# A block's rows split into halves behind the search, and one of two row sets scaled on GpSimd from the other's transposed tiles

## The chip, the cores and the metric

The kernel runs on one core of a Trainium2 chip. The metric is the device time of one execution in microseconds (us). Engines: PE is TensorE (matmuls and transposes), ACT is ScalarE, DVE is VectorE, POOL is GpSimd, and SP is the engine whose queue issues most DMAs.

## The reference, cut to what matters

Layer 0 is a graph attention layer over 2708 nodes with 512 features; layer 1, which the change concerns, is a diffusion in two steps. With h the normalised output of layer 0:

```python
S = S + eye(n)
Rf = S / S.sum(axis=1, keepdims=True)        # rows by row sums
Rb = S / S.sum(axis=0)[:, None]              # the same rows by column sums
Xf = Xb = Xa = h
for s in range(2):
    A = adj_from_feats(Xa, W1, W2, W3)       # nucleus-filtered softmax rows
    Xf = Rf @ Xf
    Xb = Rb @ Xb
    Xa = A @ Xa
    Z = Z + (Xf @ U1[s] + Xb @ U2[s] + Xa @ U3[s])
```

`adj_from_feats` forms the logits of each row (a product with 2708 keys), finds for each row the threshold above which 90% of the softmax mass lies, and keeps only what is above it. In step 0, Xf and Xb start from the same h, so both are the one product S @ h, scaled row by row: by 1/row sum for Xf, by 1/column sum for Xb. Row t of Xb is therefore row t of Xf times (row sum / column sum).

## The kernel before, in words

The 2708 rows are 22 tiles of 128 (the last has 20), taken in 11 pairs (`pairs`); two pairs make a quad (`quads`, six, the last of two tiles). After layer 0 the loop `for s in range(STEPS)` (L914) runs the two diffusion steps. Within a step, the loop over g (L1183, from -1 to 10) is a software pipeline over the pairs. In iteration g there run:

- `lg[g+2].products()` (L513): the logits of pair g+2, on PE, copied from PSUM to the tiles p by ACT (L523);
- `search(lg[g+1])` (L598): on DVE alone, the threshold of pair g+1, in rounds of passes over p (L629), then `finish` (L798), which writes the masked rows `keep` (L730) and ends in a branch on a value read from a tile (L888 to L890). `keep` is the input of the next iteration's transposes;
- `attended(pairs[g])` (L1005): A @ Xa for pair g, in 12 steps n (two tiles, six groups of up to four key tiles). In each step PE transposes four blocks of `keep` (L1016), ACT copies them to `at` (L1020), and PE multiplies the group before (L1035);
- `mixed(pairs[g])` (L1060): the three products with U1, U2 and U3, n = 0, 1, 2, with four k each. `turned_rows` transposes the rows (L147 on PE, L149 on ACT) that the next n needs, so x0, x1 (Xf, Xb, loaded at L1001) and xa are each transposed once;
- `part(half, g+2)` (L943): the product S @ h of a quad, in step 0 spread over two iterations, 11 key tiles c in each. One `product(c)` is 8 matmuls (L967) and two loads. When the second half is done, that is in odd g, `scaled` runs eight times for the quad: ACT reads a PSUM bank q and scales it by rinv or cinv into xe (L977), POOL stores xe to xfb_d (L978), and in step 0 `split_rows` (L175) follows: DVE writes a high part and the rest into split_hl (L181, L182), and POOL stores it to fhl_d or bhl_d, from which step 1 reads.
- `exp` (L526) of pair g+2: after DVE's row maxima (L548), on ACT a first pass and the exponential of each tile (L553, L560), POOL's starting points (L565 to L575), then twelve "looks" (L553), ACT passes over p of 128x2708, and POOL's `masses` (L578 to L580), on which the next search waits (L646).

The order on PE, ACT, DVE and SP is written by hand (`manual_schedule`, L1164): each engine takes its instructions in the order in which the Python code makes them. The order on POOL is found by the scheduler. Two lists are spread over `attended` and `mixed`: `others` holds the steps of `part` (11 products, in odd g of step 0 the eight `scaled` after them, and the loads of `diffused`), `fills` the ACT work of `exp`. `paced(list, n)` runs the next n entries. In `attended`, step 0 runs `1 + i` entries of `others` in each step (i is 0 for the first tile of the pair, 1 for the second) and from step `first` on one or two of `fills`; `mixed` runs one of `others` for each k, and one of `fills` for k below 3 of n = 0 and 1. What is left of both runs after `mixed`. `late` (L1220), which holds `attended` and `mixed`, comes in the code before `finish(0)` (L904, L905): what it puts on DVE stands ahead of the end of the search.

Buffers that matter: xe has 4 buffers in step 0 and 2 in step 1, split_hl 2, the PSUM tiles t (transposes and logits) 2, the PSUM tiles a (attended and mixed) 2, q one for each of the quad's four tiles, u_k 3 in step 0.

Of the kernel before, what the change touches and what calls it, by code (L numbers as in the profile page):

```python
# [24 lines left out]
P = 128  # L25
# [28 lines left out]
def kernel(  # L54
# [58 lines left out]
    xfb_d = dram.tile([2, N, D], F32, name="xfb_d")  # L113
    xa_d = dram.tile([N, D], F32, name="xa_d")
    en_d = dram.tile([H, N], F32, name="en_d")
    rank_d = dram.tile([NT * P], BF16, name="rank_d")

    ident = const.tile([P, P], F32, name="ident")
# [6 lines left out]
    rinv = const.tile([P, NT], F32, name="rinv")  # L125
    cinv = const.tile([P, NT], F32, name="cinv")
    ratio = const.tile([P, NT], F32, name="ratio")

    def row_bcast(ap, n):
        return bass.AP(tensor=ap.tensor, offset=ap.offset, ap=[[0, P], [1, n]])  # L130
# [323 lines left out]
    for r, c0, c1 in [(P, 0, NFULL), (rows[-1], NFULL, NT)]:  # L454
        if c0 == c1:
            continue
        s = (slice(0, r), slice(c0, c1))
        for v, inv in ((rsum, rinv), (csum, cinv)):
            nc.vector.tensor_scalar(v[s], v[s], 1.0, 1e-12, op0=OP.add, op1=OP.max)
            nc.vector.reciprocal(inv[s], v[s])  # L460
        nc.vector.tensor_mul(ratio[s], cinv[s], rsum[s])

# [451 lines left out]
    for s in range(STEPS):  # L914
        last = s == STEPS - 1
        with ExitStack() as st:
# [26 lines left out]
            def part(half, b):  # L943

                if b // 2 >= len(quads):
                    return []
                quad = quads[b // 2]  # L950
                first = b % 2 == 0
                w = len(quad) * P
                hl_d = (fhl_d if first else bhl_d) if last else vhl_d
                cs = range(NT) if last else range(0, NT // 2) if first else range(NT // 2, NT)
                steps = []

                def product(c):
                    if c == 0:
                        half[:] = [ps_s.tile([P, D], F32, name=f"q{i}") for i in range(len(quad))]
                    hl = sp.tile([P, 2, D], F32R, name="hl", bufs=3)  # L960
                    nc.sync.dma_start(out=hl.bitcast(F32), in_=hl_d[c * P:(c + 1) * P])
                    s_r = sp.tile([P, 2 * G * P], F32R, name="s_r")
                    nc.sync.dma_start(out=s_r[:, :w].bitcast(F32),
                                      in_=s_d[c * P:(c + 1) * P, quad[0] * P:quad[0] * P + w])
                    for j in range(len(quad)):
                        for h in range(2):
                            nc.tensor.matmul(half[j], lhsT=s_r[:, j * P:(j + 1) * P], rhs=hl[:, h],  # L967
                                             start=(c == 0 and h == 0), stop=(c == NT - 1 and h == 1))

                def scaled(t, ps, i, inv, to):  # L970
                    pr = rows[t]

                    if last and b < 2 and t % 2:
# [3 lines left out]
                    nc.scalar.activation(x[:pr], ps[:pr], AF.Copy, scale=inv[:pr, t:t + 1])  # L977
                    nc.gpsimd.dma_start(out=xfb_d[i, cols[t], :], in_=x[:pr])  # L978
                    if not last:
                        split_rows(parts, nc.vector, x[:pr], t, to)  # L980

                steps += [lambda c=c: product(c) for c in cs]
                if last or not first:
                    for j, t in enumerate(quad):
                        if first or not last:
                            steps.append(lambda j=j, t=t: scaled(t, half[j], 0, rinv, fhl_d))
                        if not first:
                            steps.append(lambda j=j, t=t: scaled(t, half[j], 1, cinv, bhl_d))
                return steps

            def paced(steps, n):
                for step in steps[:n]:
# [1 line left out]
                del steps[:n]  # L994

            def diffused(grp):
                out_ = []
                for i in range(2):
                    for t in grp:
                        x = work.tile([P, D], F32, name=f"x{i}")  # L1000
                        nc.sync.dma_start(out=x[:rows[t]], in_=xfb_d[i, cols[t], :])  # L1001
                        out_.append(x)
                return out_[:len(grp)], out_[len(grp):]

            def attended(grp, keep, rden, fills, others, then, first=3):  # L1005

# [20 lines left out]
                for n, (i, t, cs) in enumerate(steps):  # L1027
                    pr = rows[t]
                    nxt = turned(*steps[n + 1]) if n + 1 < len(steps) else then()
                    if n >= first:  # L1030
                        paced(fills, 1 + i if last else 1 if n > 8 else 2)
                    if cs[0] == 0:
                        pa = ps_a.tile([P, D], F32, name="a")
                    for j, c in enumerate(cs):
                        nc.tensor.matmul(pa[:pr], lhsT=at[:rows[c], j, :pr], rhs=va[:rows[c], c, :],  # L1035
                                         start=(c == 0), stop=(c == NT - 1))
                    if not last:
                        paced(others, 1 + i)
                    elif i or len(grp) == 1:
                        paced(others, (total + 10) // 13)  # L1040
                    if cs[-1] == NT - 1:
                        xa.append(work.tile([P, D], F32, name="xa"))
                        nc.scalar.activation(xa[i][:pr], pa[:pr], AF.Copy, scale=rden[:pr, i:i + 1])  # L1043
# [16 lines left out]
            def mixed(grp, v_t, xf, xb, xa, others, fills, final=False):  # L1060

# [6 lines left out]
                    for i, t in enumerate(grp):  # L1068
                        project(small, ps_t.tile([P, 512], F32, name="t"), v_t[i], t, s + 1)
                for n, u in enumerate((u3, u1, u2) if final else (u1, u2, u3)):  # L1070
                    nxt = turned_rows(grp, ((xf, xb) if final else (xb, xa))[n]) if n < 2 else None
                    for k in range(KD):
                        u_k = up.tile([P, D], F32, name="u_k", bufs=4 if last else 3)
                        nc.sync.dma_start(out=u_k, in_=u[s, k * P:(k + 1) * P, :])  # L1074
# [89 lines left out]
            with tc.manual_schedule(engines={PE, ACT, DVE, SP}):  # L1164
# [12 lines left out]
                for step in part(half, 0):  # L1177
                    step()
                values()
                done = []  # L1180
                ready = None
                looks, left = [], []
                for g in range(-1, NP):  # L1183

                    fills = []

                    held = len(left)
                    paced(left, held if last else held // 2)
                    others = left + part(half, g + 2)
                    left = []  # L1190
                    if g == 0 and last:
                        paced(others, 4)
                    if g + 2 < NP:
                        lg[g + 2].products()
                    if g + 3 < NP:
# [4 lines left out]

                    rows_in = []
                    if g >= 0:
                        others.insert(0 if g else len(others) // 3, lambda g=g: rows_in.extend(diffused(pairs[g])))
                        final = g == NP - 1 and not last
                        att = attended(pairs[g], *ready, fills, others,
                                       lambda: None if final else turned_rows(pairs[g], rows_in[0]),
                                       3 if g else len(tgroups) + 1)
                    if g == 0:

                        paced(others, held - held // 2 if not last else 0)  # L1210
                        while looks:
                            next(att)
                            paced(looks, 2)

                    def early(g=g):
                        if g + 2 < NP:
# [3 lines left out]
                    def late(g=g):  # L1220
                        if g >= 0:
                            if g:
                                paced(others, 1)
                            xa, v_t = rest_of(att)
                            done.extend(mixed(pairs[g], v_t, *rows_in, xa, others, fills, final))
# [52 lines left out]
```

## Time and profile before

| | |
|---|---|
| time, median of 3 runs | 3710.2 us (3706.47 to 3715.27) |
| profiled execution, its own time | 3708.3 us |
| its span, first to last instruction | 3706.5 us |
| layer 0 | 0 to about 1080 us |
| step 0 of the diffusion | about 1080 to 2300 us |
| step 1 | about 2300 to 3706 us |
| busy PE / DVE / ACT / POOL | 3367.4 / 2612.9 / 1541.5 / 799.6 us |
| mean granted TensorE clock | 0.966 of full speed |

In the tables of groups a row gives the line, the engine, out<-in, the count, the busy time, the mean of one instruction, and the idle time of the engine before it with what ended it. In a timeline the first number is the start, the second the length, and the square bracket the idle time of that engine just before, with the instruction that released it. "DVEq L890" is DVE's branch at the end of a search.

### The profile page before, as it was taken

To read this page: it belongs to the slowest core of one execution; us is meant where nothing else is said; L and a number is where in the kernel's file an instruction comes from. 1 tells how busy PE (TensorE), PEld (TensorE's weight loads), DVE (VectorE), ACT (ScalarE), POOL (GpSimd) and SP (SyncE) were. 2 spreads that over 40 slices of the span, in tenths; PEclk is the share of its full clock that TensorE was granted. 3 is DMA by queue.
4 is the path that set the end of the run, shared out by engine and by line. 5 is a ranking of instruction groups with operands and counts; after the bars stand their busy time and mean duration, and the time that the engine had idled before them with its cause. 6 is when DMAs were issued, how large, how long until landed. Compare 5 with 4: busy or idle time off the path is not lost. (4 is left out here: it accounts for less than half of the span.)

```text
span 3706.5 us, 35338 instructions
## 1 busy us (share of the span) xinstructions
PE 3367.4 (91%) x11143; PEld 1754.4 (47%) x11143; DVE 2612.9 (70%) x4820; ACT 1541.5 (42%) x2334; POOL 799.6 (22%) x1119
## 2 busy tenths in 40 slices
PE   7998999998966988989899899688999999999898
PEld 4433333333444545545455453445655565556452
DVE  4588888889957637365463651969988779777991
ACT  2343212111114674655666612345654556445511
POOL 4114140514331112121202121302112111121101
PEclk9999999999978999999999999999999999999999
DMA  3477424233228445454535353966556665566552
GB/s 113 152 252 243 137 80 150 80 105 103 74 87 278 164 157 187 145 183 149 205 131 196 128 191 100 302 203 225 175 187 208 233 216 204 183 213 234 201 201 66
DMA packets 276459, 634.08 MB, mean 171 GB/s; under 512 B 37210, under 2 KB 70442, under 8 KB 273244
## 3 DMA queue, kind: packets, MB, share of 16 engines
q1 hardware_dynamic: 249183, 540.99, 44.2%
q0 software_dynamic: 27024, 90.30, 6.3%
q8 instruction: 89, 1.46, 0.2%
q14 instruction: 163, 1.33, 0.1%
HBM read 509.07 MB, written 122.10 MB: 170 GB/s over the span
## 5 line engine op out<-in xcount | busy, mean ns | idle before, releaser
L1035 PE MATMUL a<-va,at 128*128 128x512 f32 (+2 forms) x1936 | 890.1, 599 | 14.0 <-ACT at L1020 13.5
L967 PE MATMUL q<-hl,s_r 128*128 128x512 f32 x2904 | 820.9, 429 | 62.5 <-DMA s_r<-s_d 62.2
L429 PE MATMUL po<-e,fw 128*65 128x512 f32 (+4 forms) x2112 | 838.7, 552 | 34.3 <-DVE e L427 21.8
L427 DVE SCALAR_TENSOR_TENSOR e<-r_b,kk,a_c 128x512 f32<-128x512 f32 (+4 forms) x1056 | 751.8, 741 | 73.5 <-PE po L429 23.7
L967 PEld LDWEIGHTS q<-hl,s_r 128*128 128x128 f32 x2904 | 544.4, 190 | 307.5 <-issue 133.2
L553 ACT ACTIVATE junk_a<-p,nth 128x2708 uint8<-128x2708 f32 (+1 forms) x240 | 613.1, 2554 | 70.6 <-POOL nth L572 66.8
L429 PEld LDWEIGHTS po<-e,fw 128*65 128x65 f32 (+1 forms) x2112 | 286.2, 140 | 546.7 <-issue 269.2
L1035 PEld LDWEIGHTS a<-va,at 128*128 128x128 f32 (+2 forms) x1936 | 337.1, 187 | 379.4 <-issue 342.7
L1076 PE MATMUL a<-u_k,v_t 128*128 128x512 f32 (+1 forms) x1056 | 489.9, 601 | 22.3 <-ACT xa L1043 15.4
L629 DVE SCALAR_TENSOR_TENSOR junk<-p,th 128x2708 bf16<-128x2708 f32 (+1 forms) x132 | 401.2, 3039 | 4.0
L1020 ACT COPY at<-t 128x512 f32<-128x512 f32 (+3 forms) x308 | 140.4, 477 | 494.5 <-PE t L1016 494.1
L1076 PEld LDWEIGHTS a<-u_k,v_t 128*128 128x128 f32 (+1 forms) x1056 | 188.9, 187 | 242.1 <-issue 182.9
L521 PE MATMUL t<-keys,q_t 128*128 128x452 f32 x528 | 167.1, 443 | 118.4 <-ACT p L523 98.1
L181 DVE TENSOR_SCALAR split_hl<-xe 128x512 int32<-128x512 int32 (+1 forms) x44 | 19.1, 434 | 257.1 <-ACT xe L977 210.7
L808 DVE MAX8 vn<-keep 128x8 f32<-128x2708 f32 (+1 forms) x66 | 196.8, 2981 | 2.3
L523 ACT COPY p<-t 128x452 f32<-128x452 f32 (+2 forms) x264 | 132.0, 538 | 126.5 <-PE t L521 82.3
L521 PEld LDWEIGHTS t<-keys,q_t 128*128 128x128 f32 x528 | 91.7, 211 | 189.2 <-ACT p L523 150.7
L411 ACT ACTIVATE s_c<-a_c 128x512 fp32r<-128x512 f32 (+3 forms) x132 | 76.1, 577 | 247.5 <-DMA a_c<-in_adj_t_dram 120.7
L1016 PE MATMUL t<-ident,keep 128*128 128x128 f32 (+1 forms) x968 | 147.2, 274 | 27.1 <-DVE keep L757 19.2
L1016 PEld LDWEIGHTS t<-ident,keep 128*128 128x128 f32 (+1 forms) x968 | 115.0, 139 | 107.5 <-issue 79.5
L548 DVE TENSOR_REDUCE nmx<-p 128x1 f32<-128x2708 f32 (+1 forms) x44 | 129.0, 2966 | 41.7 <-ACT p L523 41.7
L565 POOL TENSOR_TENSOR x<-sums,powers 128x4 f32<-128x4 f32 x22 | 44.7, 2033 | 508.7 <-ACT p L560 508.7
(296 smaller groups left out, 3151.9 us busy)
## 6 DMA issues: line engine op xcount, KB each, us to landing
s_r<-s_d SPq DMA_DIRECT2D x330, 256.0 KB
hl<-vhl_d SPq DMA_DIRECT2D x132, 512.0 KB
u_k<-in_L_gnn_U_dram SPq DMA_DIRECT2D x264, 256.0 KB
hl<-fhl_d SPq DMA_DIRECT2D x132, 512.0 KB
hl<-bhl_d SPq DMA_DIRECT2D x132, 512.0 KB
arow<-in_adj_dram SPq DMA_DIRECT2D x21, 1354.0 KB
s_d<-s_c SPq DMA_DIRECT2D x88, 256.0 KB
a_c<-in_adj_t_dram SPq DMA_DIRECT2D x84, 256.0 KB
```

The lines of the kernel that those rows point to most:

```text
L427: nc.vector.scalar_tensor_tensor(e[:pr, :cw], r_b[:pr, i, :cw], kk[:pr, t, hd:hd + 1], a_c[t][:pr, :cw], op0=OP.max, op1=OP.mult)
L429: nc.tensor.matmul(po[i][:, :cw], lhsT=fw[:pr, t, hd, :], rhs=e[:pr, :cw], start=(t == 0), stop=(t == NT - 1))
L521: nc.tensor.matmul(pl[:, :c1 - c0], lhsT=q[:, i], rhs=self.keys[:, c0:c1], start=(i == 0), stop=(i == 1))
L523: nc.scalar.copy(p[:pr, c0:c1], pl[:pr, :c1 - c0])
L553: nc.scalar.activation(junk[:pr], self.p[i][:pr], func, **kw)
L629: v.scalar_tensor_tensor(junk_b[:pr], ps_[i][:pr], th, ps_[i][:pr], op0=OP.is_ge, op1=OP.mult, accum_out=dst)
L808: v.max(vs, keep[0][:pr])
L967: nc.tensor.matmul(half[j], lhsT=s_r[:, j * P:(j + 1) * P], rhs=hl[:, h], start=(c == 0 and h == 0), stop=(c == NT - 1 and h == 1))
L1016: nc.tensor.transpose(pt[:rows[c], j, :pr], keep[i][:pr, cols[c]], ident[:pr, :pr])
L1020: nc.scalar.copy(at[:r, j0:j1, :pr], pt[:r, j0:j1, :pr])
L1035: nc.tensor.matmul(pa[:pr], lhsT=at[:rows[c], j, :pr], rhs=va[:rows[c], c, :], start=(c == 0), stop=(c == NT - 1))
L1076: nc.tensor.matmul(pz[i][:rows[t]], lhsT=v_t[i][:, k, :rows[t]], rhs=u_k, start=(n == 0 and k == 0), stop=(n == 2 and k == KD - 1))
```

## The change

In step 0:

- Only Xf is stored to xfb_d and loaded again by `diffused`. The column-scaled rows xe of the second kind are still made, since they are split for step 1.
- Xb's transposed tiles are formed by a new helper, `times`: GpSimd multiplies Xf's transposed tiles by a row of ratios (row sum / column sum) that is broadcast to all partitions. The ratios are transposed once behind layer 0 (PE, ACT), stored to rat_d by SP, and loaded for each pair.
- `part` returns the products and the `scaled` entries apart, and `scaled` returns its split as a function that is called later. The first half of a quad's `scaled` entries run on ACT at the end of `mixed` in odd g (`half_scaled`), ahead of the copies yo; their splits run at the top of the next iteration, behind the search. The second half and its splits run there too, behind the next pair's logits and ahead of its search.
- The pacing in `attended` is one entry of `others` in two steps of three in place of `1 + i`; in even g from 2 on, `fills` begin at step 5 in place of 3, and the loads of `diffused` stand third in `others`. The rest of `others` runs in `mixed`.

In step 1 only one order changes: what is left of `others` after the last k now runs ahead of the copies yo (L1089) in place of behind them.

```diff
+    with tc.tile_pool(name="rat", bufs=1) as pool, tc.tile_pool(name="rat_ps", bufs=1, space=PSUM) as ps:
+        pt = ps.tile([NT, P], F32, name="ratio_t")
+        nc.tensor.transpose(pt, ratio, ident)
+        ratio_t = pool.tile([NT, P], F32, name="ratio_t")
+        nc.scalar.copy(ratio_t, pt)
+        nc.sync.dma_start(out=rat_d.rearrange("(t p) -> t p", p=P), in_=ratio_t)
...
-                    nc.gpsimd.dma_start(out=xfb_d[i, cols[t], :], in_=x[:pr])
-                    if not last:
-                        split_rows(parts, nc.vector, x[:pr], t, to)
+                    if last or i == 0:
+                        nc.gpsimd.dma_start(out=xfb_d[i, cols[t], :], in_=x[:pr])
+                    return lambda: None if last else split_rows(parts, nc.vector, x[:pr], t, to)
...
+                if not last:
+                    ratios = small.tile([P, G * P], F32, name="ratios")
+                    nc.sync.dma_start(out=ratios[:, :len(grp) * P],
+                                      in_=row_bcast(rat_d[grp[0] * P:(grp[-1] + 1) * P], len(grp) * P))
-                for i in range(2):
+                for i in range(2 if last else 1):
...
-                        paced(others, 1 + i)
+                        paced(others, 1 if n % 3 else 0)
...
+            def times(grp, v_t, ratios):
+                out_ = []
+                for i, t in enumerate(grp):
+                    pr = rows[t]
+                    x = up.tile([P, KD, P], F32, name="v_t")
+                    nc.gpsimd.tensor_tensor(x[:, :, :pr], v_t[i][:, :, :pr],
+                                            ratios[:, i * P:i * P + pr].unsqueeze(1).to_broadcast([P, KD, pr]), op=OP.mult)
+                    out_.append(x)
+                return out_
...
-                    nxt = turned_rows(grp, ((xf, xb) if final else (xb, xa))[n]) if n < 2 else None
+                    if n == 2:
+                        nxt = None
+                    elif not last and n == final:
+                        nxt = times(grp, v_t, xb)
+                    else:
+                        nxt = turned_rows(grp, ((xf, xb) if final else (xb, xa))[n])
...
+                also()
                 out_ = []
...
-                    held = len(left)
-                    paced(left, held if last else held // 2)
-                    others = left + part(half, g + 2)
-                    left = []
+                    if g == 0:
+                        scaled_and_split(left, len(left) if last else len(left) // 2)
+                    others, scales = part(half, g + 2)
...
+                    if last:
+                        others += scales
+                        scales = []
+
+                    split(held)
...
-                        others.insert(0 if g else len(others) // 3, lambda g=g: rows_in.extend(diffused(pairs[g])))
+                        others.insert(len(others) // 3 if g == 0 else 2 if left else 0, lambda g=g: rows_in.extend(diffused(pairs[g])))
...
-                                       3 if g else len(tgroups) + 1)
+                                       len(tgroups) + 1 if g == 0 else 5 if left else 3)
...
+                    else:
+                        scaled_and_split(left, len(left))
+                    left = scales
+
+                    def half_scaled():
+
+                        paced(others, len(others))
+                        if g > 0:
+                            for step in left[:len(left) // 2]:
+                                held.append(step())
+                            del left[:len(left) // 2]
```

More of the change, by code (lines that the diff above doesn't have):

```diff
@@ L115 @@
     en_d = dram.tile([H, N], F32, name="en_d")
+    rat_d = dram.tile([NT * P], F32, name="rat_d")
     rank_d = dram.tile([NT * P], BF16, name="rank_d")
@@ L127 @@
     ratio = const.tile([P, NT], F32, name="ratio")
+    nc.vector.memset(ratio, 0.0)
     def row_bcast(ap, n):
@@ L948, in part @@
                 if b // 2 >= len(quads):
-                    return []
+                    return [], []
                 quad = quads[b // 2]
@@ L985, in part @@
                         if first or not last:
-                            steps.append(lambda j=j, t=t: scaled(t, half[j], 0, rinv, fhl_d))
+                            scales.append(lambda j=j, t=t: scaled(t, half[j], 0, rinv, fhl_d))
                         if not first:
-                            steps.append(lambda j=j, t=t: scaled(t, half[j], 1, cinv, bhl_d))
-                return steps
+                            scales.append(lambda j=j, t=t: scaled(t, half[j], 1, cinv, bhl_d))
+                return steps, scales
             def paced(steps, n):
@@ L1002, in diffused @@
                         out_.append(x)
-                return out_[:len(grp)], out_[len(grp):]
+                return out_[:len(grp)], out_[len(grp):] if last else ratios
             def attended(grp, keep, rden, fills, others, then, first=3):
@@ L1058, in turned_rows, with mixed @@
                 return [transposed(up, ps_t, v[i], rows[t], "v_t") for i, t in enumerate(grp)]
-            def mixed(grp, v_t, xf, xb, xa, others, fills, final=False):
+            def times(grp, v_t, ratios):
[7 more added lines that the diff above has]
+                return out_
+            def mixed(grp, v_t, xf, xb, xa, others, fills, final, also):
                 pz = [ps_a.tile([P, D], F32, name="a") for _ in grp]
@@ L1176 @@
                 lg[1].queries()
-                for step in part(half, 0):
-                    step()
+                for steps in part(half, 0):
+                    paced(steps, len(steps))
                 values()
@@ L1181, with split, scaled_and_split @@
                 ready = None
-                looks, left = [], []
+                looks, left, held = [], [], []
+                def split(rows_):
+                    for row in rows_:
+                        row()
+                    del rows_[:]
+                def scaled_and_split(scales_, n):
+                    for step in scales_[:n]:
+                        step()()
+                    del scales_[:n]
                 for g in range(-1, NP):
                     fills = []
-                    held = len(left)
-                    paced(left, held if last else held // 2)
-                    others = left + part(half, g + 2)
-                    left = []
+                    if g == 0:
+                        scaled_and_split(left, len(left) if last else len(left) // 2)
+                    others, scales = part(half, g + 2)
                     if g == 0 and last:
                         paced(others, 4)
+                    if last:
+                        others += scales
+                        scales = []
+                    split(held)
                     if g + 2 < NP:
@@ L1206 @@
                                        lambda: None if final else turned_rows(pairs[g], rows_in[0]),
-                                       3 if g else len(tgroups) + 1)
+                                       len(tgroups) + 1 if g == 0 else 5 if left else 3)
                     if g == 0:
-                        paced(others, held - held // 2 if not last else 0)
+                        scaled_and_split(left, len(left))
                         while looks:
@@ L1213 @@
                             paced(looks, 2)
+                    else:
+                        scaled_and_split(left, len(left))
+                    left = scales
[5 more added lines that the diff above has]
+                            del left[:len(left) // 2]
                     def early(g=g):
@@ L1224, in late @@
                             xa, v_t = rest_of(att)
-                            done.extend(mixed(pairs[g], v_t, *rows_in, xa, others, fills, final))
+                            done.extend(mixed(pairs[g], v_t, *rows_in, xa, others, fills, final, half_scaled))
                             paced(others, len(others))
```

## The prediction

> **What bounds the kernel now.** I read the page's busy times, then PE's and DVE's waits, then the timelines of PE, ACT and DVE over two iterations of step 0 (g=2 and 3). A groups row first, from the whole kernel:
>
> ```profile
> PE 3367.4 (91%) x11143; PEld 1754.4 (47%) x11143; DVE 2612.9 (70%) x4820; ACT 1541.5 (42%) x2334; POOL 799.6 (22%) x1119
> ...
> L181 DVE TENSOR_SCALAR split_hl<-xe 128x512 int32<-128x512 int32 (+1 forms) x44 | 19.1, 434 | 257.1 <-ACT xe L977 210.7 <-DMA bhl_d<-split_hl 27.2 <-DMA fhl_d<-split_hl 7.8
> ```
>
> PE is the bound, so a gain must be time in which PE waits or works. DVE waits 257 us ahead of the splits, yet that is no gain by itself: DVE does not end the iteration everywhere. PE's timeline shows where it does:
>
> ```profile
> 1413.40 1.95 PE L160 MATMUL t<-v_t,kw 128*128 128x128 f32 x16
> ...
> 1424.75 7.97 PE L521 MATMUL t<-keys,q_t 128*128 128x452 f32 x20 [8.20 <-ACT p L523]
> ...
> 1524.27 1.12 PE L521 MATMUL t<-keys,q_t 128*128 128x452 f32 x4 [0.74 <-ACT p L523]
> ...
> 1532.13 3.70 PE L1035 MATMUL a<-va,at 128*128 128x512 f32 x8 [0.24 <-ACT at L1020]
> ...
> 1600.01 7.97 PE L1076 MATMUL a<-u_k,v_t 128*128 128x512 f32 x14 [2.33 <-ACT xa L1043]
> ```
>
> At the start of an even g (1424.75) PE waits 8.20 us for ACT's copies of logits; at that of an odd g (1524.27) only 0.74. DVE tells why, in g=3:
>
> ```profile
> 1586.65 0.43 DVE L181 TENSOR_SCALAR split_hl<-xe 128x512 int32<-128x512 int32 x1 [42.79 <-ACT xe L977]
> ...
> 1605.65 0.43 DVE L181 TENSOR_SCALAR split_hl<-xe 128x512 int32<-128x512 int32 x1 [2.88 <-DMA bhl_d<-split_hl]
> 1606.72 3.03 DVE L806 SCALAR_TENSOR_TENSOR keep<-p,th 128x2708 f32<-128x2708 f32 x1
> ...
> 1638.02 0.17 DVE L907 RECIPROCAL rden<-den 128x2 f32<-128x2 f32 x1 [5.18 <-issue]
> ```
>
> The splits stand ahead of `finish` in DVE's order. They hold it until 1606.72, the search ends after PE has run dry (about 1625), and ACT's copies, which stand behind the branch of L890 in the next block, come late:
>
> ```profile
> 1424.16 0.97 ACT L523 COPY p<-t 128x452 f32<-128x452 f32 x2 [7.36 <-DVEq L890]
> ```
>
> **What the Trainium skill says.** (1) "TensorE: Matmul & The Clock Gate", "Part 1: The HAM clock gate": about 3.4 us without work halves TensorE's clock, about as much work restores it. The trace agrees: in the 3 us windows from 1415 the granted clock is 1.00, then 0.85, then 0.50 for 1421–1430, then 0.95. (2) "DMA: Bandwidth & Descriptors", "Anatomy of one DMA": some 2 us are fixed, most of it the receipt of the write. The trace has 3.0 us: an fhl_d store issued at 1201.18 frees its buffer at 1204.19. (3) "GPSIMD Engine Reference", section 3.1: a two-input operation there costs about twice VectorE's; the trace has 1.34 us (L1093) for 128x512.
>
> **The change part by part.** Sum against the profiled execution, 3708.3 us.
>
> *The wait at even g (g=2, 4, 6, 8).* It is 8.20, 7.92, 10.95 and 6.37: 33.4. The half clock behind it makes 20 logit products take 7.97 in place of 6.52 (1524.27 to 1530.79): 4×1.45 = 5.8. With the splits gone from behind the scales, DVE's search is no longer last. In their place come PE's usual 0.74 and four of the scales (L977) on ACT ahead of yo, 0.57 apart (1589.54, 1590.11): 3.0 in all, 12.1 for four. Net −33.4−5.8+12.1 = **−27.1**. If the search is late all the same, this is at worst 0: a rival below.
>
> *Other waits on the scales.* In odd g scales now stand ahead of xa (L1043), whence PE's 2.33 at 1600.01, four times: 9.3. Small waits on u_k follow them, 5.6 in all, for the stage's DMA has the splits' stores in it: **−14.9** (between −9.3 and −14.9).
>
> *The second four scales and splits.* They now stand on ACT behind the next pair's logits and ahead of its copies `at`. In g=0 the trace has this very order:
>
> ```profile
> 1202.32 0.69 ACT L977 ACTIVATE xe<-q,rinv 128x512 f32<-128x512 f32 x1
> ...
> 1205.43 0.69 ACT L977 ACTIVATE xe<-q,rinv 128x512 f32<-128x512 f32 x1 [1.84 <-issue]
> 1206.85 0.69 ACT L977 ACTIVATE xe<-q,cinv 128x512 f32<-128x512 f32 x1 [0.73 <-DVE split_hl L182]
> 1207.44 1.06 ACT L1020 COPY at<-t 128x512 f32<-128x512 f32 x2
> ```
> ```profile
> 1208.07 5.57 PE L1035 MATMUL a<-va,at 128*128 128x512 f32 x8 [4.94 <-ACT at L1020]
> ```
>
> split_hl has two buffers, so the third split waits for a store to land, and the scale that needs its xe waits with it. Behind the waiting scale stand `at`, the looks, and so PE. From the last logit copy to PE's first product it is 1202.43 to 1208.07 = 5.64, against 0.96 (1531.17 to 1532.13); less 0.4 that the first scales overlap, +4.3; the eight products then took 5.57 for 3.70, +1.9. So 6.2, four times: **+24.8**. Bounds: 1.9 (the four's own time on ACT, 4×0.57 less the 0.4, with no wait for a store and the clock kept) to 10 (POOL's queue: the split's stores now stand behind two additions yo, 1.3 each, and the y_d stores, all issued by POOL ahead of them). Four times, 8 to 40. DVE's search starts behind these splits, about 24 us after the boundary, and needs about 58 (as in g=3): over at 82 of some 105. I count no more for it. The last quad has two tiles, so from g=9 to 10 there are two scales ahead of yo and two ahead of `at`, four times 0.57: **+2.3**.
>
> *A look left over.* In even g the `fills` begin at step 5 in place of 3, and the order of instructions shows one of twelve looks behind yo, ahead of the next logit copies: two looks take 5.23, one with its pitch 2.67, at the start of g=3, 5, 7, 9: **+10.7** (0 to 10.7; five such looks at the start of g=1 in before make a wait of 13.95).
>
> *Pacing.* `others` go one each in two of three steps. A step of `attended` without a product q takes 3.86 us on PE, one with 5.71. ACT needs 5.8 in a step with two looks and its `at`. In steps without q ACT is then the slower by 1.9. Also the looks start later, and nth, which ACT waits for, comes 6.6 us behind the second full pass (1463.27 to 1469.86):
>
> ```profile
> ACT junk_a L553 <- POOL nth L572: 66.8, 15, 9.4
> ```
>
> Going through the new order step by step I find PE waiting 1.9 for `at` in an even g (step 10) and 3.1 in an odd one (1.1 in step 8, 2.0 in step 10): 4×1.9 + 4×3.1 = **+20.0**. Bounds: 0 (the tile `at` is made one step ahead, which may absorb it) to 42 (nth at 9.4, below). The q products themselves only move: 0.
>
> *Transposes of x1.* Removed: 1.04 to 1.09 us per pair on PE (1494.78, 1497.66), eleven pairs: **−12.0**. Their 22 copies on ACT, 22 loads on SP's queue and 22 stores on POOL's go with them; PE waits for none of these: 0. In place come two multiplications per pair on POOL, at 1.3 to 1.8 us (L1093's two rows); one took 4.0 at most, where DVE works beside it. The product that needs them is one n later, 7 us of U products or more: **0**. In the last pair the cover is just that 7 to 8 us; without it, up to 2 us × 11 = 22, which I give little weight.
>
> *Before step 0.* SP's store of the ratios waits for an ACT copy behind the last key copy (1088.75) and stands ahead of the first loads of keys, issued at 1078.98 now. PE waits till 1098.13 for q_t anyway: 0 to 3, **+1**. *Step 1*: what was left of `others` moves ahead of yo. There PE waits 1.44 at a boundary for ACT either way: 0 (−4 to +4).
>
> Sum: −27.1−14.9−12.0 = −54.0; +24.8+2.3+10.7+20.0+1.0 = +58.8; together +4.8, so 3713.1 against the profiled 3708.3. That execution lies 1.9 under the median of the runs, 3710.2; against it 3715.0. The gains are spent again: the same work on ACT stands in PE's way at another place.
>
> **The rivals.** *ScalarE becomes the bound in the second half of `attended`* (slower). Mechanism: looks start two steps later and are as many, so all now depends on when nth comes. At 6.6 us behind the second full pass it is as counted; POOL now has `times`, yo and the splits' stores to do in the same stretch. From 7.5 us on each us goes to PE, and at before's longest, 9.4, it is 2.8×8 = 22: about 3737. For it: the measured 9.4, POOL's strict queue. Against: POOL is busy 22% only. A search that is late in spite of all (from 22 us more on DVE) would end here too, near 3750; the margin speaks against it. *ScalarE keeps up* (faster): `at` is made ahead, the pacing's 20 falls to 0, and PE keeps its clock behind the second scales (4×1.9 = 7.6 less): 3715−27.6 = about 3688, with the left-over look still paid. For it: PE's waits for `at` are 13.5 in the whole kernel now. Against: g=0 shows the loss of clock.
>
> **How the numbers follow.** Forecast case 0.45, slower rival 0.30, faster rival 0.25. 0.2%, or 7.4 us, is about what a measurement of this kernel can tell from no change. The forecast's own range is 3703 to 3727, of which I give 0.30 to within 0.2%, 0.12 above, 0.03 below; the slower rival lies all above; of the faster one 0.02 is within. So faster 0.26, same 0.32, slower 0.42. The range runs from the faster rival, 3688, to 3742, where the pacing's upper bound is joined by some of the boundary's.
>
> **What would show it.** Right: the branch of L890 no longer releases the copies p; PE's wait at even boundaries is about 3 us at full clock, then 4 to 5 us for `at` and a half clock; one look lies between yo and the logit copies before odd g; waits of 1 to 3 us for `at` in steps 8 to 10; L147 has 264 transposes of x in place of 352; step 1 is as long as before. Wrong: PE waits for neither `at` nor p (the faster rival), or ACT's wait for nth grows with PE's wait for `at` (the slower), or the p copies still wait for L890.

## The result and the profile after

| | before | after |
|---|---|---|
| median (4 runs each) | 3711.0 us | 3746.7 us (3743.8 to 3755.3) |
| ratio | | 1.0102, 95% interval 1.009 to 1.0114 |
| span of the profiled execution | 3706.5 | 3753.0 |
| mean granted clock | 0.966 | 0.957 |

The change makes the kernel 1.0% slower, 36 us, and 5 us above the upper end of the prediction's whole range (3688 to 3742). The page's first row (busy time, share, instructions):

```profile
PE 3389.7 (90%) x11056; PEld 1760.4 (47%) x11056; DVE 2606.8 (69%) x4821; ACT 1534.7 (41%) x2313; POOL 829.0 (22%) x1119
```

PE is busy for 22 us longer with 87 instructions fewer in the row: it ran at a lower clock.

The two profiled spans differ by 46.5 us. Cut at the first logit product (L521 before, L530 after) of each iteration, that is: 5.4 before step 0 begins, 30.1 in step 0, 4.8 in step 1, and 6.3 behind the last output store. The first and third pieces are no more than scatter: in the profiles cut in this way step 0 begins between 1092 and 1104 us, and step 1 takes 1391 to 1400 us up to the last output store. (The profiled execution is the longest of the four, 9 us above their median.) The last piece is not scatter; it comes again below. Within step 0:

| us | up to g=1 | g=1 | g=2 | g=3 | g=4 | g=5 | g=6 | g=7 | g=8 to the end |
|---|---|---|---|---|---|---|---|---|---|
| before | 199.8 | 117.2 | 107.0 | 103.3 | 106.2 | 101.9 | 109.5 | 104.3 | 259.9 |
| after | 196.5 | 113.7 | 109.4 | 103.6 | 116.0 | 103.6 | 115.1 | 103.6 | 277.8 |

Odd iterations are as long as before. The even ones and the end of the step lose. PE's timeline over g=4 shows where (from the column in brackets one reads the idle time ahead of the instruction and what ended it):

```profile
1631.10 7.29 PE L530 MATMUL t<-keys,q_t 128*128 128x452 f32 x20 [3.04 <-ACT p L532]
...
1646.73 1.22 PE L977 MATMUL q<-hl,s_r 128*128 128x512 f32 x2 [5.81 <-ACT xe L987]
...
1700.87 6.47 PE L1052 MATMUL a<-va,at 128*128 128x512 f32 x8 [3.77 <-ACT at L1037]
...
1747.30 4.81 PE L530 MATMUL t<-keys,q_t 128*128 128x452 f32 x12 [3.25 <-ACT p L532]
```

At the same place of the kernel before, PE waited 7.92 for copies p that stood behind the branch of L890:

```profile
1634.79 7.52 PE L521 MATMUL t<-keys,q_t 128*128 128x452 f32 x20 [7.92 <-ACT p L523]
```

It is 3.04 now, as forecast. In its place stand three other waits. First, 5.81 for a bank q, which a scale on ACT has yet to read. That scale (L987) waits 4.60:

```profile
1644.73 0.69 ACT L987 ACTIVATE xe<-q,rinv 128x512 f32<-128x512 f32 x1 [4.60 <-issue]
```

The view names no releaser for it. That it waits for a buffer xe, which the third split frees at 1644.65, is read from GpSimd's and VectorE's timelines, and the run with six xe below takes the wait away:

```profile
1632.64 2.61 POOL L1126 TENSOR_TENSOR yo<-yo,va 128x512 f32<-128x512 f32 x2
1635.09 1.16 POOL L1128 DMA_DIRECT2D y_d<-yo  x2
1636.18 0.60 POOL L186 DMA_DIRECT2D fhl_d<-split_hl  x1
```
```profile
1643.50 0.43 DVE L184 TENSOR_SCALAR split_hl<-xe 128x512 int32<-128x512 int32 x1 [12.78 <-DMA fhl_d<-split_hl]
```

The first split was done at 1629.1, but its store stood in GpSimd's queue until 1636.18, behind work on the keys, two stores of xe, the two additions yo and their stores. The third split, which waits for its buffer, began 7.3 us after that issue. Second, 3.77 us for `at`, because ACT, which copies it, stands at the first look, which waits for nth:

```profile
1695.03 2.55 ACT L562 ACTIVATE junk_a<-p,nth 128x2708 uint8<-128x2708 f32 x1 [6.67 <-POOL nth L581]
```
```profile
1686.47 3.08 POOL L574 TENSOR_TENSOR x<-sums,powers 128x4 f32<-128x4 f32 x1 [5.18 <-ACT p L569]
...
1691.96 3.03 POOL L581 TENSOR_SCALAR nth<-th_a 128x6 f32<-128x6 f32 x1
```
```profile
1685.61 3.04 DVE L815 SCALAR_TENSOR_TENSOR keep<-p,th 128x2708 f32<-128x2708 f32 x1
...
1691.85 3.03 DVE L815 SCALAR_TENSOR_TENSOR keep<-p,th 128x2708 f32<-128x2708 f32 x1
```

L574 takes 1.04 us in g=2 and L581 0.26:

```profile
1472.56 1.04 POOL L574 TENSOR_TENSOR x<-sums,powers 128x4 f32<-128x4 f32 x1 [5.18 <-ACT p L569]
...
1477.96 0.26 POOL L581 TENSOR_SCALAR nth<-th_a 128x6 f32<-128x6 f32 x1
```

In g=4 both began inside one of VectorE's passes L815, and ended 0.9 and 0.1 us behind it. The Trainium skill ("GPSIMD Engine Reference", section "8. Key points") says that GpSimd shares its SBUF interfaces with VectorE, in contention with instructions of two SBUF inputs; L815, which reads p twice, is one. The trace agrees: of 62 GpSimd instructions that began inside a two-input pass of VectorE of some 3 us, 59 ended with it or later (two of the other three only write), but of 76 that began inside a MAX8 pass as long, which has one input, 73 ended before it did. So nth came 8.7 us after the second full pass (1686.38 to 1695.03). In g=2 one instruction between the two shown is caught by a pass as well, and nth comes after 5.8. I call a chain "held" when a pass catches L581 too, as here and in g=6 and 8, and "free" otherwise. Third, 3.25 us for the look left over behind yo.

Each of these waits is followed by work at half the clock (the windows 1645.10:1648.40, 1699.70:1706.40 and 1747.50:1750.80 have 0.50): 6.47 us in place of 3.70 at 1700.87. From g=2 to the end of step 0 the mean granted clock is 0.95, before it was 0.98. In the waits of the whole kernel:

```profile
PE a L1052 <- ACT at L1037: 43.5, 25, 7.8
...
PE q L977 <- ACT xe L987: 19.8, 6, 6.0
```

Before, the second was not there, and the first was

```profile
PE a L1035 <- ACT at L1020: 13.5, 19, 4.9
```

### The profile page after: what moved, and what is told of

The parts are those of the page before. It is cut to its first block, busy times and chain, and to the rows that moved or that the text cites. A ratio compares the mean times of both kernels' runs of the same rounds, so it can differ in the third digit from the quotient of the medians.

```text
span 3753.0 us, 35175 instructions
## 1 busy us (share of the span) xinstructions
PE 3389.7 (90%) x11056; PEld 1760.4 (47%) x11056; DVE 2606.8 (69%) x4821; ACT 1534.7 (41%) x2313; POOL 829.0 (22%) x1119
## 5 line engine op out<-in xcount | busy, mean ns | idle before, releaser
L1052 PE MATMUL a<-va,at 128*128 128x512 f32 (+2 forms) x1936 | 907.3, 608 | 43.5 <-ACT at L1037 43.5
L977 PE MATMUL q<-hl,s_r 128*128 128x512 f32 x2904 | 834.1, 432 | 86.0 <-DMA s_r<-s_d 66.0
L562 ACT ACTIVATE junk_a<-p,nth 128x2708 uint8<-128x2708 f32 (+1 forms) x240 | 613.1, 2555 | 107.5 <-POOL nth L581 103.7
L530 PE MATMUL t<-keys,q_t 128*128 128x452 f32 x528 | 173.1, 457 | 94.6 <-ACT p L532 79.4
L532 ACT COPY p<-t 128x452 f32<-128x452 f32 (+2 forms) x264 | 134.2, 541 | 104.4 <-PE t L530 88.4
L530 PEld LDWEIGHTS t<-keys,q_t 128*128 128x128 f32 x528 | 94.7, 217 | 168.7 <-ACT p L532 137.6
```

Source lines behind the costliest of these rows:

```text
L530: nc.tensor.matmul(pl[:, :c1 - c0], lhsT=q[:, i], rhs=self.keys[:, c0:c1], start=(i == 0), stop=(i == 1))
L532: nc.scalar.copy(p[:pr, c0:c1], pl[:pr, :c1 - c0])
L562: nc.scalar.activation(junk[:pr], self.p[i][:pr], func, **kw)
```

## The experiments

Medians are set against the 3746.7 of the changed kernel; the kernel before gave 3707 to 3711 beside them, so a difference of 4 us or less between runs taken apart can't be read. Iterations are cut as above. "Even" is g=2, 4, 6; "odd" is g=3, 5, 7.

**Six buffers xe** (and the ratios in one, to make room).

```diff
-bufs=2 if last else 4)
+bufs=2 if last else 6)
```

> The changed kernel with six buffers xe in place of four (ratios in one buffer to make room). The last two of the four scales behind the logits then no longer need a split, and so no landed store, to get a buffer. Theory: ACT waits there for xe, and through q's banks and the copies at PE stands 5.4 to 7.8 us four times, at half the clock after it: the time falls by some 7 us at each of four boundaries, 28 in all, from 3747 to about 3719. Rival (the loss is in the second half of attended, where ACT waits for nth): at most 5 us less, about 3742.

3727.0, ratio to before 1.0053 (1.004 to 1.0066): 20 less, between the two. The wait for q is gone, as the theory said, but even iterations are 110.9, 111.0 and 111.6, no shorter than the free g=2 of the changed kernel, 109.4. The time comes back where fills begin, in ACT's and PE's timelines of this kernel in g=4:

```profile
1669.72 0.20 ACT L565 ACTIVATE nmx<-nmx 128x1 f32<-128x1 f32 x1 [7.23 <-DVE nmx L557]
```
```profile
1676.38 6.47 PE L1052 MATMUL a<-va,at 128*128 128x512 f32 x8 [6.30 <-ACT at L1037]
```

The row maxima stand on VectorE behind the splits, and the splits still wait for their stores. The nth chains of all even g are free in this profile (L574 1.04, L581 0.26), and that may account for the gain; it isn't shown, since in the two profiles step 0 is only 9.9 us shorter, and the rest of their difference lies in the two pieces that are scatter. So the wait for xe is real, but taking it away lets PE run into the next.

**The ratios alone, on the kernel before** (loads, block and `times` as in the change's diff; nothing else of it).

> The kernel before with one part of the change alone: only Xf is stored to xfb_d and loaded again, Xb's transposed tiles are made on GpSimd by times, and the ratios are written behind layer 0. Splits, scales, pacing and looks are those of before. Theory (this part saves what it takes off PE, and the changed order is what costs): eleven pairs of transposes at 1.09 are 12 us less, the store of the ratios ahead of the keys 5 us more, about 3704. Rival (GpSimd's multiplications beside VectorE's passes are late for the products, or slow the search): 3715 or more.

3736.1, ratio 1.0074 (1.0061 to 1.0087): the rival. In g=3 the multiplications stand among the splits on both engines:

```profile
1600.64 3.15 DVE L184 TENSOR_TENSOR split_hl<-xe,split_hl 128x512 f32<-128x512 f32 x1
```
```profile
1600.75 2.49 POOL L1078 TENSOR_TENSOR v_t<-v_t,ratios 128x512 f32<-128x512 f32 x2
```
```profile
1644.67 4.91 PE L529 MATMUL t<-keys,q_t 128*128 128x452 f32 x12 [13.10 <-ACT p L531]
```

The split's subtraction takes 3.15 us in place of 0.69 and the stores behind it wait for GpSimd, so the search ends later and PE's wait at the boundary is 13.1 in place of 7.9. The products that use the multiplied tiles were never late. What was late is what stands behind the multiplications. (6 of the 29 us are at the end of the span, for a reason that comes below.)

**Looks behind the third n of mixed.**

```diff
-                        if n < 2 and k < 3:
+                        if (n < 2 or not last) and k < 3:
```

> The changed kernel with looks also behind the third n of mixed in step 0 (three more places for fills), so that no look is left over behind yo. Theory: the wait of 3.25 us at the start of g=3, 5, 7, 9 falls to about 0.7 and the half clock after it, 0.9, goes: 4 x 3.4 = 14 less, about 3733. Rival (ACT has no slack there, and the look stands in the way of the key copies instead): no change, 3747.

3715.7 over 14 runs (3699.6 to 3726.0), ratio 1.0018 (1.0006 to 1.0029): 31 less, twice the theory's. Odd iterations fall from 103.6 to 98.4; PE's wait at the start of g=5 is 0.73. That is 5.2 each, of which the look's 2.5, up to 0.9 of the clock's and 1.5 less waiting for `at` explain nearly all. The theory left out g=1, where five looks stood ahead of the logit copies: it falls from 113.7 to 104.4, a quarter of what step 0 gains between the two profiles. Even ones are 109.3, 110.5 and 109.9, with all three chains free. In the changed kernel's profile two of these three are held, and most of the rest of the gain is there; how often a chain is held varies from run to run, which is in keeping with these runs' wide spread, though there is the trace of only one.

**The first look one step later** (two empty places behind the starting points in even g, besides the edit above).

```diff
-                steps.append(lambda: None)
+                steps += [lambda: None] * (1 if self.s or grp[0] // G % 2 else 3)
```

> As the kernel with looks behind the third n, and besides two empty places behind the starting points in even g, so that the first look, which waits for nth on ACT, comes one step later, behind the next copies at. Theory: PE's waits of 3.8, 4.2 and 4.7 us for at in g=4, 6, 8 come from ACT standing at nth while GpSimd's chain is held up by VectorE's passes; with the half clock after them they are 20 us: about 3713 (14 + 20 less than 3747). Rival (ACT is simply full in these steps): about 3733, as without the empty places.

3710.2 over 13 runs (3703.2 to 3715.5), ratio 1.0005 (0.9996 to 1.0014): near the theory's 3713, but not because of the empty places. Both numbers took the kernel with looks alone to be at 3733; it is at 3715.7, and what the empty places add is 5 us, well under the theory's 20. The trace tells more than the median. Here the chains are held in every even g, and it costs nothing: in g=4 ACT waits 0.80 for nth, and even iterations are 110.5, 111.3 and 109.8, as with free chains.

```profile
1685.19 3.04 POOL L581 TENSOR_SCALAR nth<-th_a 128x6 f32<-128x6 f32 x1
```
```profile
1688.26 2.55 ACT L562 ACTIVATE junk_a<-p,nth 128x2708 uint8<-128x2708 f32 x1 [0.80 <-POOL nth L581]
```

**The change without the ratios**, and the same with looks behind the third n.

> The changed kernel without the part with the ratios: both kinds of rows are stored and loaded again, and PE transposes x1 as before; the split splits, the pacing and the looks are those of the change. Theory (in the old order that part cost 29 us because its multiplications stood on GpSimd ahead of the splits' stores; in the new order no split stands there): the transposes come back, 11 x 1.09 = 12 us more, about 3758. Rival (GpSimd's multiplications cost as much wherever they stand): some 29 us less, about 3718.

> As the kernel without the ratios, and with looks also behind the third n of mixed. With the earlier run of the looks (3716 with the ratios) it makes a square of two by two. Theory: the ratios save their 12 us here too, about 3728. Rival: 3690.

3749.8 and 3722.4, against 3746.7 and 3715.7 with the ratios. The rival falls; the ratios cost nothing in the new order, but what they save is 3 us, which can't be told from nothing, and 7, not 12. In both profiles chains are held in all three even g: these iterations take 116.9 to 117.9, where held ones of the changed kernel take 115.1 and 116.0; odd ones take 104.8, 104.8 and 105.3 (first kernel), against 103.6. That is 1.2 to 1.9 per pair, all that the transposes are worth (1.09). So it is lost again elsewhere, below.

**Step 1 as before.**

```diff
-                        paced(others, len(others))
+                        if not last:
+                            paced(others, len(others))
```

> The changed kernel with the order of step 1 put back: what is left of others runs behind the copies yo there, as before. Theory (the new order lets PE and ACT meet better at each boundary of step 1: 116.1 us for an iteration in place of 116.65): 7 x 0.5 = 4 us more, about 3750, and iterations of 116.6 in the trace. Rival (step 1 is the same either way): 3747.

3746.2 (3743.7 to 3753.6), no difference. Most iterations of step 1 are 116.66 in this trace and 116.1 in the changed kernel's, so the effect exists, 0.5 each, but is too small to be seen in the median (one iteration of the changed kernel's is 119.0). Its step 0 is the changed kernel's, and here the other chains are held: even iterations are 114.7 (held), 109.6 (free) and 116.6 (held). A held chain costs about 6 us.

**The old pacing.**

```diff
-                        paced(others, 1 if n % 3 else 0)
+                        paced(others, 1 + i)
```

> The changed kernel with the old pacing in attended: one entry of others in each step of the first tile, two in each of the second. Theory of the forecast (the new pacing leaves steps without a product, in which ACT is the slower): the waits for at go, 20 to 25 us less, about 3724. Rival (the wait is for nth alone, held up on GpSimd by VectorE's passes, whatever PE has to do): within 6 us of 3747.

3728.0, ratio 1.0057 (1.0043 to 1.0071): 19 less, near the theory, and the forecast's term of 20. No wait for `at` is left in g=4, even iterations are 110.8, 110.0 and 110.3, odd ones 102.6, 102.0 and 102.0. With two products in each step of the second tile PE has work while ACT stands at nth, even in g=6, where L581 took 3.01.

**Three edits together: six xe as above, looks behind every k of mixed, fills of even g from step 6.**

```diff
-                        if n < 2 and k < 3:
+                        if not last or (n < 2 and k < 3):
...
-len(tgroups) + 1 if g == 0 else 5 if left else 3)
+len(tgroups) + 1 if g == 0 else 6 if left else 3)
```

> The changed kernel with three edits together: six xe (no scale waits for a split), looks behind every k of all three n of mixed, and in even g the fills from step 6 in place of 5, so that ACT doesn't stand at the row maxima that VectorE, held by the splits, delivers late. Theory (the loss is ACT standing in PE's way at three places, xe, nth and the left-over look): below both kernels, about 3690. Rival (taking one wait away lets PE run into the next, as when six xe alone brought 20 of 28 us): as with the looks alone, 3710 to 3716.

3678.8, ratio 0.9918 (0.9904 to 0.9931): faster than both kernels, and 11 below the theory. Even iterations are 103.7, 104.4 and 105.2, odd ones 99.3. Taken apart:

> The fast joint kernel (3679) with xe back at four buffers. Theory (PE stands 5.4 to 7.8 us at four boundaries, with the half clock 7 each, and nothing behind gives it back): 28 more, about 3707. Rival (a part comes back, since VectorE's row maxima are as late with six as with four): 8 to 20 more, 3687 to 3699.

> The fast joint kernel (3679) with the fills of even g from step 5 again. Theory (with six xe PE comes to step 5 before the row maxima are there, and ACT stands at them and at nth in front of the copies at): waits for at of some 5 us in g=2, 4, 6, with the half clock 7: 20 more, about 3699. Rival (the looks' new places in mixed bring it all): 3679.

With four xe 3696.0 (ratio 0.9971, 0.9963 to 0.9979), even iterations of 108.8 to 109.0: 17 more, inside the rival's bounds. With fills from step 5 3704.1 (0.9986, 0.9979 to 0.9993), even iterations of 111.5 to 112.9: 25 more, above the theory's 20; PE waits 8.06 for `at` in g=4, behind ACT's 8.99 for the row maxima:

```profile
1658.09 0.20 ACT L565 ACTIVATE nmx<-nmx 128x1 f32<-128x1 f32 x1 [8.99 <-DVE nmx L557]
```

Only when both ends of the stretch are loosened is the wait for xe worth its 5 us per iteration.

**The joint kernel with four xe, without the ratios.**

> The joint kernel with four xe (3696), without the part with the ratios: rows of both kinds stored and loaded, x1 transposed on PE. Here the waits for nth and the left-over look are gone, so the part is measured with little of either beside it. Theory (the ratios are worth the transposes that they take off PE, 11 x 1.09, and GpSimd's multiplications are hidden): 12 more, about 3708. Rival (GpSimd's multiplications cost elsewhere what the transposes save): 3696 or less.

3703.2 over 21 runs, against 3696.0: the ratios are worth 7, between theory and rival. The rest of the transposes' 12 is at the end of the span. In the changed kernel the last row of GpSimd's timeline, and the page's head:

```profile
3742.90 0.54 POOL L1142 DMA_DIRECT2D out_dram<-yo  x1 [0.76 <-DVE yo L1141]
```
```profile
span 3753.0 us, 35175 instructions
```

The span ends 10.1 us behind the issue of the last output store. Before it was 3.8 (to 3706.5):

```profile
3702.72 0.53 POOL L1109 DMA_DIRECT2D out_dram<-yo  x1 [0.76 <-DVE yo L1108]
```

It is 9.9 to 10.1 in every profile of a kernel with the ratios shown so far and 3.7 to 3.8 in every one without. Three kernels, each run once, looked for the piece that does it:

> The joint kernel with four xe and without the ratios (3703, end 3.8 us behind the issue of the last store), with only the block behind layer 0 put in: the ratios are transposed, copied and stored by SP, and nothing reads them. If that block brings the late end, the end is 10.1 us behind the last store; if not, 3.8.

> The same with the block and with the loads of the ratios for each pair, which nothing reads; the rows x1 are loaded and transposed as before. If the broadcast loads bring the late end, it is 10.1 us behind the last store; if it is 3.8 here too, the multiplications on GpSimd (with the rows of x1 no longer stored and loaded) bring it.

> The joint kernel with four xe and with the ratios (3696), with the 22 stores of the column-scaled rows put back, which nothing reads. If GpSimd's lower number of stores brings the late end, the span ends 3.7 to 3.8 us behind the issue of the last output store here; if the multiplications bring it, 10.1.

3.7 in all three (times of 3699.4, 3703.1 and 3698.1). The last one has everything of the ratios but issues the 22 stores of the column-scaled rows again; so it is their absence that brings the late end:

```profile
3692.61 0.53 POOL L1142 DMA_DIRECT2D out_dram<-yo  x1 [0.76 <-DVE yo L1141]
```
```profile
span 3696.3 us, 35234 instructions
```

Why fewer stores on GpSimd's queue make the end later, no view here shows.

> The fast joint kernel (3679) with the 22 stores of the column-scaled rows put back, which nothing reads. Theory: the span ends 3.7 us behind the last store in place of 10.1, and the stores are hidden: 3672 to 3673. Rival (the stores delay those of the splits on GpSimd's queue, and so the row maxima): 3679 or more.

3677.2 (3673.9 to 3679.8), ratio 0.9915 (0.9901 to 0.9928), against 3678.8: the end is 3.7, but step 0 is 3.5 us longer and step 1 1.9, so the two can't be told apart, and the theory's 6 us do not show.

## Why the prediction was wrong

The direction of the mechanism was right ("the same work on ACT stands in PE's way at another place"), the sum too small by 32 us. The largest miss is the size of one term, the second four scales: 24.8 forecast, about 35 measured. The step that was wrong in kind is the delay of nth, taken as 6.6 us and measured at 8.7. By the steps, each read from the one profile of a kernel:

- *The wait at even g*, −27.1: right in the waits. PE waits 3.04 at all four; L890 releases none of them. Only the clock is not full behind them: 20 logits took 7.3 in g=2 and 4 and 7.9 to 8.0 in g=6 and 8, in place of 6.52, so that 4 of the 5.8 to be gained from the clock did not come.
- *Other waits on the scales*, −14.9: right. PE's waits for xa went from 15.4 to 5.3, those for u_k from 6.7 to 1.8, together 15.0.
- *The second four scales*, +24.8: mechanism right, size too small, though inside the bounds (8 to 40). PE waits 6.9, 6.7 and 6.2 in g=2, 4, 6 (with 0.86 at the scale before) and 7.84 in g=8, 27.6 in all; with slow transposes and products behind (1.91 and 4.87 for 1.06 and 3.70 in g=4, 2.0) this is about 35. GpSimd's queue, named only as an upper bound, is one half of the reason: 7 us from the split to its store's issue. The other is the landing, read as 3.0 from g=0: here the third split began 7.3 after the issue. With 3.0 it would have begun at about 1639.2, when the scales did (1638.86); that is an estimate from these lines, and no run separates the two.
- *A look left over*, +10.7: the wait is as forecast, 3.25 less 0.74. Its removal saved 5.2 per odd iteration, about twice the term, because some of the clock and of the waiting for `at` went with it.
- *Pacing*, +20.0: PE's waits for `at` in these places add up to 22.3, 2.4 of which stood in g=8 before too, so the total fits; the places do not. It was to be 1.9 in each even g and 3.1 in each odd one. Measured are 2.6 in g=3, 5 and 7 and none in g=9; 0.9 in g=2; and 3.8 to 4.7 in g=4, 6 and 8, with 1.7 to 3.0 of slow clock behind each, 7 in all, which was not counted. That the total came out is luck. "nth comes 6.6 us behind the second full pass" is the step that failed: it came after 8.7. The slower rival had the mechanism (nth late, PE waits for `at`) and 22 us for it, but put it down to GpSimd's own queue; VectorE's passes held it.
- *Transposes*, −12.0, and *multiplications*, 0: right on PE and in this order. But the 22 stores on GpSimd that "PE waits for none of" were counted at 0, and without them the span ends 6.3 us later. And where splits stand behind the multiplications (the kernel before), they cost more than all that is saved; the forecast asked only whether the product that needs them is late, not what stands behind them on GpSimd.
- *The last quad*, +2.3: measured 3.28 at the start of g=9 and 3.02 at that of g=10, each with 5.40 in place of 3.70 behind it, 9.7; with the look's 2.7 added the forecast had 5.
- *Before step 0*, +1, and *step 1*, 0: within scatter.

The profile of before had a sign of what became of nth. Its 6.6 in g=2 already contains one pass: L565 took 3.72 there, beginning inside L806, and 1.04 in g=3. In g=4 of the changed kernel the chain meets two. And the 9.4 that the slower rival took for the longest delay was an idle time of ACT in step 1 (at 2406 us), not a delay behind a full pass.

```profile
1463.24 3.03 DVE L806 SCALAR_TENSOR_TENSOR keep<-p,th 128x2708 f32<-128x2708 f32 x1
...
1463.46 3.72 POOL L565 TENSOR_TENSOR x<-sums,powers 128x4 f32<-128x4 f32 x1 [38.02 <-ACT p L560]
```
```profile
1561.52 1.04 POOL L565 TENSOR_TENSOR x<-sums,powers 128x4 f32<-128x4 f32 x1 [30.85 <-ACT p L560]
```

The excess over the forecast is thus some 4 of clock behind the even waits, 10 at the second scales, 7 of clock behind the held chains, 6 at the end, and 5 in the last quad. These overlap, as the runs with six xe show, and add up to the 32 only roughly. The run with the old pacing, 19 less, is no proof of the term of 20 either: it takes the waits for `at` away, but brings one of 0.88 for xa into each iteration.

## What to carry to other kernels

When a wait is moved from one engine's path to another's, follow the chain one link further than the wait: here buffer, store, the store's place in GpSimd's queue, and then the row maxima behind the splits. Here a wait removed was worth its length only where nothing else was due a few steps later; loosen both ends together, as the joint kernel did. And an instruction that others wait for should not be laid beside long two-input passes of VectorE if it is on GpSimd, or its consumer should be given a step of slack: in the run that gave it, held chains cost nothing.

## What was not expected of the hardware

- A GpSimd instruction of 0.26 us took 3.03 when it started inside a two-input pass of VectorE, and VectorE's subtraction of 0.69 took 3.15 beside GpSimd's multiplications. Beside VectorE's MAX8 pass, which has one input, L581 took 0.26 (1674.22 in the kernel with looks behind the third n, MAX8 from 1672.09 for 2.98).
- A store on GpSimd's queue freed its buffer 7.3 us after its issue, one of g=0 in the kernel before after 3.0. The stores to fhl_d took 2.9 to 9.5 us to land in the changed kernel, 3.3 in the median, and up to 6.4 before.
- PE's waits of no more than 3.04 us were followed by half the clock (1631.40:1634.80 has 0.50), and in the kernel before one of 2.33 was too (1601.00:1604.00), while others of 2.33 were not (1390.00:1393.00 and 1809.00:1812.00 have 1.00). So the 3.4 us that the prediction quotes is no safe bound in this case.
- With 22 stores fewer on GpSimd's queue the span ended 10.1 us behind the last output store, with them 3.7.
